# A four-layer image network: group norms' deviation moved to ScalarE, layer 1's front split and taken two images ahead

## The chip, the cores and the metric

The kernel runs on one core of a Trainium2 chip. The core has five engines that work from queues of their own: TensorE (PE, matrix products and transposes), VectorE (DVE), ScalarE (ACT), GpSimd (POOL) and SyncE (SP), which here issues all DMA transfers. An engine takes its instructions in order; an instruction waits on semaphores for the results of other engines, and everything behind it on its engine waits with it. The metric is device time in microseconds (us) of one execution.

## The reference

The input is 16 images of 192 channels by 32 x 32 points in float32. Four layers follow, each of the form `x = x + layer(group_norm(x))` with 32 groups of 6 channels. A group norm takes the mean and the variance over a group's channels and all points, and gives `(x - mean) / sqrt(var + 1e-5)`; "the deviation" below is the factor `(var + 1e-5) ** -0.5`.

- Layer 0 is an mLSTM block over the 1024 points as a sequence, then a 3 x 3 convolution, then a batch norm over all images and a leaky ReLU.
- Layer 1 is a Mamba block: layer norm, input projection to 384 channels and a gate, a causal convolution of width 4, SiLU, a selective scan with 16 states, gating, output projection, `skip_scale * xf` added, layer norm, projection.
- Layer 2 is a depthwise 3 x 3 convolution, batch norm over all images, clip to 0..6.
- Layer 3 is a vision Mamba with four scan directions per image beside a depthwise branch.

The recurrence that takes most of the time is, per state n and channel d, `h = exp(dt * A[d, n]) * h + dt * x * B[n]`, with `y += h * C[n]`.

The batch norm of layer 0 needs all images, so its leaky ReLU and the sum with x are done when layer 1 begins an image; the layer 1 group norm comes right after it. That beginning is called the front.

## The kernel before

Channels lie on partitions: 192 channels as two tiles of 96 (`m`), 384 as three of 128 (`t`). The 1024 points are two halves of 512. Layer 0 runs over all images first, then layers 1 and 2 together, then layer 3.

The scan of layers 1 and 3 (`scan_run`) goes over units, a unit being one half of one image (and direction), and over the 16 states of each: one pair is a step. Layer 1 has 32 steps an image, 512 in all; layer 3 has 2048. In a step ScalarE multiplies the transposed input by B (L966, tile `xbt`) and makes the decays (L986, `da`, five buffers), TensorE transposes the products into PSUM (L994, L997, `xb`, three buffers), VectorE runs three scan instructions (L1010, `h`), GpSimd multiplies by C (L1017), and TensorE adds up the result over states by transposes into PSUM (L1028, `y`). The row of C comes by DMA, broadcast to all partitions (`cb`, L968, four buffers).

All other work of layers 1 to 3 is written as generators and woven into the scan by `Side`. Each task has a kind, a start and an end, counted in steps; at every third of a step `tick` advances a task so far that its share of yields fits the time gone. A `Wait(n)` in a generator keeps it from going on for n steps. The tile framework then orders each engine's instructions and adds the semaphores.

In layer 1 image b begins at step `at = 32 * b`. Its neighbours' work is woven in: `prep` (projection to dt, B, C, and the transposes for the next unit), `gate` (gated output of the unit just done), `out` (output projection of image b-1), `silu` (the gate z of image b from its normalized input `xn`), `front` (for image b+1), `tail` (image b-1: layer norm, projection, sum with x1, group norm for layer 2), `conv` (causal convolution of image b+1, ending in a SiLU), and `layer 2` (image b-1). A SiLU on ScalarE needs another table of functions; `silu` (L1280s) loads it and then loads the table with logarithm and exponential again, so it is three instructions (L1283 twice, L1284).

The front of one image (`layer1_front`) has these parts: load x (`x1`, one buffer) and the layer 0 result (`xf`, one buffer) by DMA; batch norm's scale and shift on ScalarE (L1233), leaky ReLU (L1234) and sum (L1235) on VectorE; store of the sum to `self.x1`; group norm; the normalized image into `xf` (L1240) and its store to `self.xf1`; layer norm into `xn`, which takes x's buffer; projection and store of `xin` in DRAM, from which `conv` reads shifted copies (`rep`). `out` loads the stored `xf1` into the tile `xt` (one buffer), and `tail` works in that tile to the end of its group norm (`xpad`, L1351).

`group_norm` (L344 to L370) takes statistics per channel on VectorE (L351, L352), averages means over a group with a tiny matrix product (L355), takes deviations of means and a second moment (L357 to L362), averages again (L365), and makes the deviation: VectorE adds epsilon (L367), GpSimd raises to the power -0.5 (`pow_mhalf`, L309). It is used by layer 0's image (L541), layer 1's front and tail, and layer 3's front. `pow_mhalf` stays in use for batch norms.

Of the kernel before, what the change touches and what calls it, by code (L numbers as in the profile page):

```python
# [10 lines left out]
F32 = mybir.dt.float32  # L11
AF = mybir.ActivationFunctionType
# [4 lines left out]
ADD, SUB, MUL, MAX, MIN, POW = ALU.add, ALU.subtract, ALU.mult, ALU.max, ALU.min, ALU.pow  # L17

C = 192
HP = 96  # L20
DI = 384
S = 1024
# [6 lines left out]
EPS = 1e-5  # L29
# [160 lines left out]
def halves(n=S, step=512):  # L190
    return [slice(i, i + step) for i in range(0, n, step)]


def finish(steps):

    while True:
        try:
            next(steps)
        except StopIteration as end:
            return end.value  # L200
# [74 lines left out]
class Program:  # L275
# [68 lines left out]
    def group_norm(self, pool, psum, x):  # L344

        nc = self.nc
        st = pool.tile([HP, 2, 2, 6], F32, name="gnst")
        mv = pool.tile([HP, 2, 2], F32, name="gnmv")
        for m in range(2):
            for i, h in enumerate(halves()):  # L350
                nc.vector.bn_stats(st[:, m, i], x[:, m, h])  # L351
            nc.vector.bn_aggr(mv[:, m], st[:, m].rearrange("p a b -> p (a b)"))  # L352
            yield 1
        ps = psum.tile([128, 512], F32, name="mm")
        nc.tensor.matmul(ps[:HP, :2], self.k("group", HP), mv[:, :, 0], start=True, stop=True)  # L355
        mean = pool.tile([HP, 2], F32, name="gnmean")
        nc.vector.tensor_copy(mean, ps[:HP, :2])  # L357
        d = pool.tile([HP, 2], F32, name="gnd")
        nc.vector.tensor_tensor(d, mv[:, :, 0], mean, SUB)
        q = pool.tile([HP, 2], F32, name="gnq")  # L360
        nc.vector.tensor_tensor(q, d, d, MUL)
        nc.vector.tensor_tensor(q, q, mv[:, :, 1], ADD)  # L362
        yield 1
        ps = psum.tile([128, 512], F32, name="mm")
        nc.tensor.matmul(ps[:HP, :2], self.k("group", HP), q, start=True, stop=True)  # L365
        r = pool.tile([HP, 2], F32, name="gnr")
        nc.vector.tensor_scalar(r, ps[:HP, :2], EPS, None, ADD)  # L367
        self.pow_mhalf(r)
        yield 1
        return mean, r, d  # L370

# [698 lines left out]
    def layer12(self):  # L1070
        tc = self.tc
        with (
            tc.tile_pool(name="w1", bufs=1) as wp,
            tc.tile_pool(name="s1", bufs=2) as sp,
            tc.tile_pool(name="b1", bufs=2) as bp,
            tc.tile_pool(name="d1", bufs=3, space=DRAM) as dp,
            tc.tile_pool(name="ps1", bufs=2, space=PSUM) as psum,
        ):
            self.layer1_weights(wp, dp, psum)
            self.rep = 18 * (W + 2), 6  # L1080
            self.stats = wp.tile([HP, 2, 2 * self.nb, 6], F32, name="stats")
            self.image = {b: {} for b in range(self.nb)}
            side, units = Side(), []
            w_x = [self.w_x[:, t] for t in range(3)]

            def prep(u):
                xt = bp.tile([128, 4, DI], F32, name="xtok", bufs=1)
                xc = self.image[u.b]["xc"]
                rows = yield from self.scan_rows(xc[:, :, 512 * u.half : 512 * u.half + 512], w_x, 1, bp, dp, psum)
                yield from self.scan_prep(u, rows, 0, xc, xt, True, self.w_dt, bp, psum)  # L1090

            carry = [wp.tile([128, NS, 3], F32, name=f"carry{i}") for i in range(2)]
            for b in range(self.nb):
                for half in range(2):
                    c = carry[b % 2]
                    u = Unit(b, half, False, False, c if half else None, None if half else c)
                    u.neg_a = lambda t, n: self.neg_a[:, t * NS + n : t * NS + n + 1]
                    u.finish = lambda y, u=u: self.layer1_sum(u, y, bp)
                    units.append(u)
            for b in range(self.nb):  # L1100
                at = 2 * NS * b
                side.add("prep", prep(units[2 * b + 1]), at + 1, at + 13)
                if b:
                    side.add("gate", self.layer1_gated(units[2 * b - 1], bp, psum), at + 2, at + 3.5)
                    side.add("out", self.layer1_out(b - 1, bp, psum), at + 3.5, at + 8)
                side.add("silu", self.layer1_gate(b, bp, psum), at + 8, at + 12.5)
                if b + 1 < self.nb:
                    side.add("front", self.layer1_front(b + 1, sp, bp, psum), at + 12.5, at + 20)
                if b:
                    side.add("tail", self.layer1_tail(b - 1, sp, bp, dp, psum), at + 13.5, at + 25)  # L1110
                side.add("gate", self.layer1_gated(units[2 * b], bp, psum), at + 18, at + 21)
                if b + 1 < self.nb:
                    side.add("conv", self.layer1_conv(b + 1, bp, psum), at + 20, at + 26)
                if b:
                    side.add("layer 2", self.layer2(b - 1, bp, psum), at + 25.5, at + 34)
                if b + 1 < self.nb:
                    side.add("prep", prep(units[2 * b + 2]), at + 26, at + 30)
            finish(self.layer1_front(0, sp, bp, psum))
            finish(self.layer1_conv(0, bp, psum))
            finish(prep(units[0]))  # L1120
            self.scan_run(units, side, bp, psum)
            finish(self.layer1_gated(units[-1], bp, psum))
            finish(self.layer1_out(self.nb - 1, bp, psum))
            finish(self.layer1_tail(self.nb - 1, sp, bp, dp, psum))
            finish(self.layer2(self.nb - 1, bp, psum))
            self.batch_norm(sp, "2gamma", "2beta", self.bn2)
# [95 lines left out]
    def layer1_front(self, b, sp, bp, psum):  # L1222

        nc = self.nc
        x = bp.tile([HP, 2, S], F32, name="x1", bufs=1)
        nc.sync.dma_start(x, self.ins["x"][b].rearrange("(m p) t -> p m t", p=HP))
        xf = bp.tile([HP, 2, S], F32, name="xf", bufs=1)
        nc.sync.dma_start(xf, self.y0[b].rearrange("(m p) t -> p m t", p=HP))
        yield Wait(1)
        for m in range(2):  # L1230
            for h in halves():
                v = xf[:, m, h]
                nc.scalar.activation(v, v, AF.Identity, bias=self.bn0[:, m, 1:2], scale=self.bn0[:, m, 0:1])  # L1233
                nc.vector.scalar_tensor_tensor(v, v, 0.01, v, MUL, MAX)  # L1234
                nc.vector.tensor_tensor(x[:, m, h], x[:, m, h], v, ADD)  # L1235
                yield 0.5
        nc.sync.dma_start(self.x1[b], x)
        mean, r, _ = yield from self.group_norm(sp, psum, x)
        for m in range(2):
            nc.vector.tensor_scalar(xf[:, m], x[:, m], mean[:, m : m + 1], r[:, m : m + 1], SUB, MUL)  # L1240
        nc.sync.dma_start(self.xf1[b], xf)
        yield 1
        xn = x
        for h in halves():
            yield from self.layer_norm(
                bp, psum, [xf[:, m, h] for m in range(2)], [xn[:, m, h] for m in range(2)],
                self.k("ones192", HP), HP, 512,
            )
        for t in range(3):
            for h in halves():  # L1250
                ps = psum.tile([128, 512], F32, name="mm")
                for m in range(2):
                    nc.tensor.matmul(
                        ps, self.w_in[:, m, t * 128 : (t + 1) * 128], xn[:, m, h], start=m == 0, stop=m == 1
                    )
                o = bp.tile([128, 512], F32, name="o")
                nc.scalar.activation(o, ps, AF.Identity, bias=self.b_in[:, t : t + 1])
                nc.sync.dma_start(self.xin[b % 2][t][:, 3 + h.start : 3 + h.stop], o)
                yield 1.7
        self.image[b]["xn"] = xn  # L1260
# [450 lines left out]
```

## Time and profile before

| | us |
|---|---|
| median of three timed runs | 17368.59 |
| the three runs | 17350.56, 17368.59, 17390.61 |
| profiled execution's own time | 17403.5 |
| its span, first to last instruction | 17401.7 |
| first and last scan of layer 1 | 3943.8, 7529.7 |
| first and last scan of layer 3 | 7767.7, 17332.3 |

| engine | busy us | share of the span |
|---|---|---|
| PE | 15749.6 | 91% |
| DVE | 13122.0 | 75% |
| ACT | 11873.6 | 68% |
| POOL | 11450.8 | 66% |

How to read the lines shown below. A line of a view by tile or line gives the kernel's line, engine, operation, names as `out<-in`, how many there are, and minimum/median/maximum duration in ns; below it stand the engine's idle time ahead of these, by what ended it, and the time that others waited for them, with counts. A line of the timeline gives start and duration in us, then the same names, merged for neighbours alike, and in brackets the idle time of the engine before it and what ended that. A line of the windows gives each engine's busy time in a stretch. Matrix products overlap in the pipeline, so a busy PE is not one at its peak.

### The profile page before, as it was taken

Reading aid. Unit: us, or ns where it says so; the run is one execution under the profiler, and the core shown is the slowest. Engines: PE = TensorE matmul, PEld = TensorE weight load, DVE = VectorE, ACT = ScalarE, POOL = GpSimd, SP = SyncE. Lnnn points to the kernel's source line nnn. Section 1 sums busy time; section 2 is a strip of 40 time slices with the busy share of each in tenths; the row PEclk is TensorE's granted clock in tenths of the full one; section 3 lists DMA queues with packets and bytes.
Section 4 is the critical chain, followed back from the end, with each engine's and each line's share of the span. In section 5 each row is a group of like instructions: output and inputs, shape, how many; then the busy total and the mean of one; then the engine's idle time right before and its main releaser. Section 6 shows DMA issues by size and latency. Waiting matters only on the chain. (4 is left out here: it accounts for less than half of the span.)

```text
span 17401.7 us, 263068 instructions
## 1 busy us (share of the span) xinstructions
PE 15749.6 (91%) x99452; PEld 11013.2 (63%) x99452; DVE 13122.0 (75%) x14859; ACT 11873.6 (68%) x19637; POOL 11450.8 (66%) x5555
## 2 busy tenths in 40 slices
PE   8998988888988899979899999999999999999998
PEld 4444444435555555547777777777777777777777
DVE  4444444437777777749889888888888888888888
ACT  3222322327666666648888888888888888888888
POOL 3333333425555555538788788888878888888888
PEclk8889998989999999989999999999999999999999
DMA  1111111123333343433333333323333333333332
GB/s 51 42 40 44 44 43 44 47 63 107 114 110 110 113 118 116 118 99 103 90 99 107 93 96 101 107 83 99 107 98 92 99 108 88 96 105 102 88 98 67
DMA packets 890141, 1544.65 MB, mean 89 GB/s; under 512 B 83472, under 2 KB 314653, under 8 KB 879530
## 3 DMA queue, kind: packets, MB, share of 16 engines
q1 hardware_dynamic: 888874, 1527.81, 30.3%
q8 instruction: 788, 12.91, 0.3%
q14 instruction: 479, 3.92, 0.1%
HBM read 1284.22 MB, written 243.27 MB: 88 GB/s over the span
## 5 line engine op out<-in xcount | busy, mean ns | idle before, releaser
L1017 POOL TENSOR_TENSOR h<-h,cb 128x1536 f32<-128x1536 f32 x2560 | 8872.8, 3469 | 1432.0 <-DVE h L1010 902.9
L986 ACT ACTIVATE da<-dt,neg_a 128x512 f32<-128x512 f32 x7680 | 5267.0, 714 | 1752.0 <-DVE h L1010 1687.3
L1010 DVE TENSOR_TENSOR_SCAN h<-da,carry,xb 128x512 f32<-128x512 f32 x3840 | 4652.4, 1262 | 657.1 <-PE xb L997 596.2
L1028 PE MATMUL y<-const,h 128*128 128x128 f32 x30720 | 4717.9, 276 | 128.3 <-DVE ysum L1468 54.0
L1010 DVE TENSOR_TENSOR_SCAN h<-da,xb 128x512 f32<-128x512 f32 x3840 | 4440.6, 1202 | 388.7 <-PE xb L997 270.7
L994 PE MATMUL xb<-const,xbt 128*128 128x128 f32 x23040 | 4074.6, 282 | 422.5 <-DVE h L1010 269.3
L966 ACT ACTIVATE xbt<-ut,bt 128x384 f32<-128x384 f32 x7680 | 4174.4, 603 | 246.4 <-PE xb L994 244.3
L994 PEld LDWEIGHTS xb<-const,xbt 128*128 128x128 f32 x23040 | 2757.2, 143 | 1815.5 <-issue 643.8
L1028 PEld LDWEIGHTS y<-const,h 128*128 128x128 f32 x30720 | 3684.9, 143 | 322.8 <-issue 265.4
L997 PE MATMUL xb<-diag,ut 128*128 128x128 f32 x15360 | 3016.4, 279 | 0.0
L997 PEld LDWEIGHTS xb<-diag,ut 128*128 128x128 f32 x15360 | 2383.5, 195 | 63.1 <-issue 63.1
L830 POOL TENSOR_TENSOR hs<-h,mhm 128x384 f32<-128x384 f32 x128 | 108.5, 848 | 1685.1 <-DVE den L835 1290.5
L1016 POOL COPY carry<-h 128x3 f32<-128x3 f32 x1280 | 250.5, 196 | 1220.1 <-DVE h L1010 964.7
L976 POOL TENSOR_TENSOR diag<-const,bt 128x512 f32<-128x512 f32 x640 | 680.8, 1064 | 550.5 <-PE xb L997 362.1
L705 POOL TENSOR_TENSOR e<-e,const 128x1536 f32<-128x1536 f32 x128 | 439.9, 3437 | 288.9 <-DMA e<-row 273.0
L520 PE MATMUL conv<-ya,w_conv 128*64 128x512 f32 (+1 forms) x1152 | 543.9, 656 | 66.1 <-DMA ya<-yrows 62.2
L916 PE MATMUL mm<-dbl,w_dt 45*128 45x512 f32 x960 | 532.8, 639 | 33.6 <-DVE v L1490 16.2
L711 ACT ACTIVATE e<-e 128x1536 f32<-128x1536 f32 x128 | 189.7, 1482 | 417.7 <-POOL e L706 417.4
L854 DVE TENSOR_TENSOR ht<-sz,mm 128x384 f32<-128x384 f32 x128 | 70.7, 552 | 519.5 <-PE mm L851 519.5
L1171 PE MATMUL mm<-rep,t_dw 96*32 96x512 f32 x2304 | 433.5, 614 | 23.5 <-DMA rep<-xr 17.3
L779 PEld LDWEIGHTS num<-v,p 128*128 128x128 f32 x3072 | 389.3, 201 | 102.2 <-issue 77.9
L920 DVE SCALAR_TENSOR_TENSOR dt<-lnsq,mm 128x512 f32<-128x512 f32 x480 | 322.0, 671 | 171.9 <-ACT lnsq L919 171.9
(272 smaller groups left out, 17910.1 us busy)
## 6 DMA issues: line engine op xcount, KB each, us to landing
cb<-row SPq DMA_DIRECT2D x2560, 256.0 KB
rep<-xr SPq DMA_DIRECT2D x384, 331.0 KB
e<-row SPq DMA_DIRECT2D x128, 768.0 KB
rep<-xin SPq DMA_DIRECT2D x384, 256.0 KB
rep<-xr SPq DMA_DIRECT2D x384, 228.8 KB
x<-x SPq DMA_DIRECT2D x48, 768.0 KB
xr<-xin SPq DMA_DIRECT2D x48, 612.5 KB
xr<-xpad SPq DMA_DIRECT2D x32, 867.0 KB
```

The source lines that it names most:

```text
L520: nc.tensor.matmul(o, self.w_c2[:k, t, c0 : c0 + o.shape[0]], src[:k, r0 : r0 + 16, dx : dx + W], start=t == 0, stop=t == 14, skip_group_c ...
L705: nc.gpsimd.tensor_tensor(k.e, k.e, self.k0("mask")[:, None, :].to_broadcast([128, NH, 128]), ADD)
L916: nc.tensor.matmul(ps, w_dt[:, t * 128 : (t + 1) * 128], dbl, start=True, stop=True)
L966: nc.scalar.activation(t[:, c], u.ut[:, c], AF.Copy, scale=u.bt[:, c, n : n + 1])
L976: nc.gpsimd.tensor_tensor(d, ident[:, None, :].to_broadcast([128, 4, 128]), u.bt[:, 3, n : n + 4][:, :, None].to_broadcast([128, 4, 128]), ...
L986: nc.scalar.activation(da[i, t], u.dt[:, t], AF.Exp, scale=u.neg_a(t, n))
L994: in_order(nc.tensor.transpose(xb[i, t][:, c * 128 : (c + 1) * 128], xbt[i][:, c, t * 128 : (t + 1) * 128], ident))
L997: in_order(nc.tensor.matmul(xb[i, t][:, 384:], u.ut[:, 3, t * 128 : (t + 1) * 128], u.diag[n // 4][:, n % 4], start=True, stop=True, skip_ ...
L1010: nc.vector.tensor_tensor_scan(hv, dv, xv, 0.0 if first else u.carry_in[:, n, t : t + 1], MUL, ADD)
L1017: nc.gpsimd.tensor_tensor(h[i], h[i], u.c.pop(n)[:, None, :].to_broadcast([128, 3, 512]), MUL)
L1028: in_order(nc.tensor.matmul(u.y[:, j], h[i][:, t, c * 128 : (c + 1) * 128], ident, is_transpose=True, start=n == 0 and j % 4 == 0, stop=n ...
L1171: self.nc.tensor.matmul(ps[32 * g : 32 * g + 32], blocks[:, g * side + r], seen, start=r == 0, stop=r == side - 1, skip_group_check=True,)
```

## The change

1. `group_norm` makes the deviation on ScalarE: `Ln(v + eps)`, then `Exp(-0.5 * that)`. The averaged variance is read from PSUM by the first of them.
2. `layer1_front` now ends with the store of the normalized image, and leaves `xf` for later. What followed it becomes a task of its own, `layer1_xin`. The layer norm's output gets the tile `x1`; the sum x is loaded into the tile `xt`, which `out` and `tail` use as well. The front yields 1 instead of 0.5 for each of its four pieces.
3. In `layer12` the front runs for image b+2 in steps 26.5 to 35 of image b (image 1's in steps 2 to 10 of image 0), and `xin` for image b+1 in steps 13 to 20. Several other tasks have their starts and ends moved: `prep`, `silu`, `tail`, `gate`, `conv`, `layer 2`.

```diff
@@ group_norm
         r = pool.tile([HP, 2], F32, name="gnr")
-        nc.vector.tensor_scalar(r, ps[:HP, :2], EPS, None, ADD)
-        self.pow_mhalf(r)
+        nc.scalar.activation(r, ps[:HP, :2], AF.Ln, bias=self.k("eps", HP))
+        nc.scalar.activation(r, r, AF.Exp, scale=-0.5)
         yield 1
@@ layer12
                 at = 2 * NS * b
-                side.add("prep", prep(units[2 * b + 1]), at + 1, at + 13)
+                side.add("prep", prep(units[2 * b + 1]), at + 0.5, at + 12)
                 if b:
                     side.add("gate", self.layer1_gated(units[2 * b - 1], bp, psum), at + 2, at + 3.5)
                     side.add("out", self.layer1_out(b - 1, bp, psum), at + 3.5, at + 8)
-                side.add("silu", self.layer1_gate(b, bp, psum), at + 8, at + 12.5)
+                elif self.nb > 1:
+                    side.add("front", self.layer1_front(1, sp, bp, psum), 2, 10)
+                side.add("silu", self.layer1_gate(b, bp, psum), at + 8, at + 13)
                 if b + 1 < self.nb:
-                    side.add("front", self.layer1_front(b + 1, sp, bp, psum), at + 12.5, at + 20)
+                    side.add("xin", self.layer1_xin(b + 1, bp, psum), at + 13, at + 20)
                 if b:
-                    side.add("tail", self.layer1_tail(b - 1, sp, bp, dp, psum), at + 13.5, at + 25)
-                side.add("gate", self.layer1_gated(units[2 * b], bp, psum), at + 18, at + 21)
+                    side.add("tail", self.layer1_tail(b - 1, sp, bp, dp, psum), at + 14, at + 26)
+                side.add("gate", self.layer1_gated(units[2 * b], bp, psum), at + 18.5, at + 22)
                 if b + 1 < self.nb:
-                    side.add("conv", self.layer1_conv(b + 1, bp, psum), at + 20, at + 26)
+                    side.add("conv", self.layer1_conv(b + 1, bp, psum), at + 18, at + 24.5)
+                    side.add("prep", prep(units[2 * b + 2]), at + 24.5, at + 29.5)
                 if b:
-                    side.add("layer 2", self.layer2(b - 1, bp, psum), at + 25.5, at + 34)
-                if b + 1 < self.nb:
-                    side.add("prep", prep(units[2 * b + 2]), at + 26, at + 30)
+                    side.add("layer 2", self.layer2(b - 1, bp, psum), at + 26, at + 35)
+                if b + 2 < self.nb:
+                    side.add("front", self.layer1_front(b + 2, sp, bp, psum), at + 26.5, at + 35)
             finish(self.layer1_front(0, sp, bp, psum))
+            finish(self.layer1_xin(0, bp, psum))
@@ layer1_front
-        x = bp.tile([HP, 2, S], F32, name="x1", bufs=1)
+        x = bp.tile([HP, 2, S], F32, name="xt", bufs=1)
...
-                yield 0.5
+                yield 1
...
         nc.sync.dma_start(self.xf1[b], xf)
+        self.image[b]["xf"] = xf
         yield 1
-        xn = x
+
+    def layer1_xin(self, b, bp, psum):
+
+        nc = self.nc
+        xf = self.image[b].pop("xf")
+        xn = bp.tile([HP, 2, S], F32, name="x1", bufs=1)
         for h in halves():
             yield from self.layer_norm(
```

## The prediction

> **What bounds the kernel now.** I read the page first: TensorE is busy 91% of 17401.7 us, VectorE 75%, ScalarE 68%, GpSimd 66%, so no engine is full and order matters. Group norms carry little work; what counts is who waits at them. The view of the group norm's deviation, limited to layer 0 (200 to 3700 us), answers that:
>
> ```profile
> L309 POOL TENSOR_TENSOR gnr<-gnr,const x15: 685/694/700, 200.3 to 3455.0; 96x2 f32<-96x2 f32 x15
>   POOL gnr L309: 55.5, 15
>   PE mm L377: 94.9, 14
> ```
>
> The power takes 0.69 us, but VectorE sits idle 55.5 us in 15 images for it (3.7 each) and TensorE 94.9 us for the normalized image behind it. The same view of layer 3's loop (7700 us on) has VectorE idle 23.7 us in 15 images (1.58 each). One layer 0 image, VectorE and GpSimd by time, shows why:
>
> ```profile
> 1372.98 0.14 DVE L367 TENSOR_SCALAR gnr<-mm 96x2 f32<-96x2 f32 x1
> 1373.05 0.54 DVE L854 TENSOR_TENSOR ht<-sz,mm 128x384 f32<-128x384 f32 x1
> 1376.55 3.80 DVE L543 TENSOR_SCALAR x<-x,gnmean,gnr 96x1024 f32<-96x1024 f32 x2 [2.96 <-POOL gnr L309]
> ...
> 1373.11 2.75 POOL L706 TENSOR_TENSOR e<-e,uw 128x1536 f32<-128x1536 f32 x1
> 1375.82 0.69 POOL L309 TENSOR_TENSOR gnr<-gnr,const 96x2 f32<-96x2 f32 x1
> ```
>
> The power stands behind a 2.75 us product in GpSimd's queue.
>
> Layer 1 is the larger part. Each of its images repeats nearly alike, 226 to 232 us from scan to scan in the timeline. I cut image 7 at its scan steps 0, 5, 12, 18, 27 and 32 (32 steps an image) and took the windows:
>
> ```profile
> core 0: us, PE busy (x) PEld busy (x) DVE busy (x) ACT busy (x) POOL busy (x), PEclk, DMA share, GB/s
> 5510.40:5536.60 26.20, 24.13 (x173) 18.86 (x172) 19.98 (x21) 19.40 (x32) 20.51 (x12) 0.93 0.22 65
> 5536.60:5585.00 48.40, 46.30 (x261) 31.33 (x260) 34.45 (x37) 32.49 (x55) 30.20 (x20) 1.00 0.16 48
> 5585.00:5628.90 43.90, 33.95 (x198) 24.89 (x197) 37.71 (x46) 30.77 (x47) 23.25 (x12) 0.92 0.31 91
> 5628.90:5703.00 74.10, 65.61 (x365) 38.92 (x363) 57.72 (x65) 44.79 (x68) 37.92 (x15) 1.00 0.59 176
> 5703.00:5741.60 38.60, 37.11 (x228) 20.59 (x227) 24.32 (x27) 29.51 (x51) 19.70 (x8) 1.00 0.50 141
> ```
>
> TensorE's idle time is the wall less its busy time: 2.1, 2.1, 9.9, 8.5 and 1.5 us. The hole is in the third row, steps 12 to 17, where VectorE is at 86%. It is the present front of the next image:
>
> ```profile
> 5595.28 4.67 DVE L1235 TENSOR_TENSOR x<-x,xf 96x512 f32<-96x512 f32 x4 [1.81 <-DMA x<-x]
> 5599.87 1.87 DVE L351 BATCH_NORM_STATS2 gnst<-x 96x6 f32<-96x512 f32 x3
> 5611.81 2.24 DVE L1240 TENSOR_SCALAR xf<-x,gnmean,gnr 96x1024 f32<-96x1024 f32 x2 [0.70 <-POOL gnr L309]
> ```
>
> Step 13 takes 13.7 us against 3.3 to 7 in quiet ones: after its three scans VectorE waits 1.81 us for x, then does sums and statistics while the next scan, and TensorE behind it, stand. ScalarE is meanwhile in silu with its two table loads (1.28 + 2.77 + 1.28 = 5.3 us), so the two holes partly cover each other.
>
> **What the Trainium skill says.** "SBUF — State Buffer", Who interferes with whom: a VectorE instruction with two SBUF inputs, or in a 2-port mode, and a GpSimd one that reads SBUF exclude each other for a whole instruction. The trace agrees: the first of the four sums at L1235 took 2.86 us, the others 0.68; gnq at L361 took 2.42 us once in image 7 instead of 0.13; xpad at L1351 3.94 instead of 0.79. "ScalarE: Activation LUTs", What ACT_TABLE_LOAD costs: about 1283 ns a load; the trace has 1283. Same page, Table sets: logarithm and exponential share one set, so the new pair should switch nothing. The built program agrees: inside the loops no load is added; only ahead of layer 0 there is one more.
>
> **The change part by part**, against the profiled execution's 17403.5 us (span 17401.7). The three timed runs' median is 17368.6, 35 below, and the sum is carried over as a difference.
>
> *Deviation on ScalarE.* Per group norm one 0.145 us VectorE instruction (L367) and a 0.69 us GpSimd power go, and two tiny ScalarE instructions come; the nearest row, the 128x12 pair at L839 and L840, takes 0.21 us each. 64 times 0.42 us is 27 us of ScalarE, which is idle 32% of the time.
>
> Layer 0: in the program's order the pair stands after L840 and ahead of the exponential at L711, where ScalarE waited 2.34 us in the image shown, so it is covered; bare it costs 0.4 an image. TensorE's order is otherwise the one of before. The deviation is there some 0.5 us after L840 begins, not behind L706. The most to win is the whole idle 3.7 us an image. The least is nothing: L543 can wait for GpSimd's 2.75 us product at the shared port instead. I take 2.0, as the power's own 0.69 certainly leaves the chain: 15 x 2.0 = -30 (0 to -55).
>
> Layer 3: orders are the same but for the group norm; the pair sits between copies of step-ahead input (L966) and xpad moves behind the third scan. VectorE's 1.58 us a front is at stake; ScalarE's place costs at most one 0.6 us instruction ahead of it. I take -1.3 x 15 = -20 (-24 to +10).
>
> Start: one table load more, +1.3.
>
> *Front split and moved.* From steps 13 to 15 go, on VectorE, four sums and their wait (6.5), four statistics (2.5), small pieces (about 1), L1240 and its wait (2.9): 13 us. In exchange xin's layer norm (L379, L389), formerly in steps 16 to 18, starts at 13, and silu is now bare: VectorE has about 3.5 us of scans in step 14 beside 5.3 of ScalarE. Decays (L986) are made ahead in five buffers, over a step, which hides most of it. Of the 9.9 us hole I let silu keep 2 and win 8 (4.6 if silu is wholly bare; 9.9 if not at all).
>
> The new place is steps 27 to 33, beside layer 2's matmuls, with TensorE idle 1.5 us in 38.6 but VectorE idle 14.3. Into it come four sums (2.7), four statistics (2.5), aggregates and 96x2 pieces (1), two normalizations (1.6): 7.8 us. The leaky ReLU (L1234, four of 0.67) and its ScalarE half stay near steps 18 and 19. VectorE's queue has scans behind each piece and TensorE waits for scans, so what VectorE's spare time doesn't cover is paid. The sums stand at four places now, each open to a port wait; before, one of 2.2 us was paid. I take +3 (0 if all is covered, +14.7 if 7.8 is bare with two port waits of 3.45).
>
> DMAs: x now loads into xt on SP after xpad's store to xr and prep's row store, ahead of layer 2's replicas; x1d and xf1d stores and the next y0 load keep their sizes. SP holds the C rows (cb) too, four buffers deep, and those queue behind any wait. The load took 7.1 us from issue (5588.2) to the release of L1235 (5595.3). From xpad in step 25 to the first sum, late in step 27, there are some 9 us, so I price lateness at 0 (up to +3, like the 1.8 paid now; layer 2's replicas would be late next). xf1d's store, the row store and xt's load at steps 1 to 2 have until step 5.
>
> The tail's group norm (step 24, 12 us) loses GpSimd's power between scans: -1 (0 to -2). Conv, prep and silu of xc move earlier by about two steps; steps 18 to 26 keep their TensorE work, so 0 (-4 to +4).
>
> Image: -8 + 3 - 1 = -6. The loop has 15 images' fronts in both kernels (image 0 gains a second, image 14 loses its own): 15 x -6 = -90.
>
> Sum: -30 - 20 - 90 + 1 = -139: 17403.5 becomes 17264, the median **17230 us** (ratio 0.992).
>
> **Rivals.**
>
> *Whole hole won*: front covered at its new place and silu by the lead of the decays: -9.9 - 1 and one or two of rebalancing, -12 an image, -180; with -65 of group norms 17124. For it: VectorE's idle 14.3. Against: port waits.
>
> *Only the norms*: layer 1 trades one hole for another, -50: 17319.
>
> *Slower: the front is bare where it lands.* Steps 27 to 33 have no idle TensorE; each VectorE microsecond ahead of a scan is paid (+14.7) and of the old hole only 4.6 comes back, as silu loses its cover: +10 an image, +150 - 50 = +100: 17469. It decides once layer 1 loses over (35 + 50)/15 = 5.7 us an image. For it: today's front shows just such a bunching. Against: the program's order spreads the pieces between scans there, where today eight stand in one gap.
>
> *Nothing*: port waits take the place of the power and layer 1 trades evenly: 17369. The change does do what it says: in the built program no power is left in a group norm's chain.
>
> **How the numbers follow.** My case (17170 to 17300) 0.44; whole hole 0.14; only norms 0.10; nothing 0.10; slower 0.22. 0.2% (35 us) is about what measuring this kernel can tell from no change. Faster: 0.44 + 0.14 + most of the norms' case = 0.66; same 0.12; slower 0.22. Range: from 17080, past the whole-hole case (its bounds reach 17070), to 17450, short of the slower case's centre.
>
> **What would show it.** Right: image to image about 224 us in layer 1; the window of steps 12 to 17 some 8 us shorter; no 13 us step there; L543's wait in layer 0 under 2 us and named for ScalarE; layer 3 shorter by about 1 us an image. Wrong: steps 27 to 33 longer by over 8 us with VectorE full, sums at 3 us (port) or waiting for x, scans waiting for decays behind silu, or cb late behind SP's stores.

## The result, and the profile after

The changed kernel takes **17205.5 us**, the median of four runs (17199.5 to 17211.1), against 17367.3 for the kernel before on the same chip: ratio 0.9906, 95% interval 0.9889 to 0.9923. It is faster by 162 us, or 0.94%.

Where the time went, from the first and last scan of each layer in the two profiles:

| us | before | after | difference |
|---|---|---|---|
| layer 0, to the first scan of layer 1 | 3943.8 | 3876.0 | -67.8 |
| layer 1, first to last scan | 3585.9 | 3480.9 | -105.0 |
| between | 238.0 | 232.8 | -5.2 |
| layer 3, first to last scan | 9564.6 | 9547.6 | -17.0 |
| end | 69.4 | 71.7 | +2.3 |
| span | 17401.7 | 17209.0 | -192.7 |

The two profiles differ by 31 us more than the medians: the profiled execution of before was 36 us above its median, that of after (17210.8) 5 us. Layer 0 varies from profile to profile: of the changed kernel and those told of below, the nine that have the new deviation and leave its small operands as they are took 3846 to 3901 us, mean 3870; the two with the old deviation (before and `e2`) took 3944 and 3926.

The view by tile of the group norm's deviation, in layer 0 (200 to 3700 us), after:

```profile
L543 DVE TENSOR_SCALAR x<-x,gnmean,gnr x30: 799/1927/3236, 209.0 to 3396.7; 96x1024 f32<-96x1024 f32 x30
L367 ACT ACTIVATE gnr<-mm,const x15: 240/241/258, 202.5 to 3393.8; 96x2 f32<-96x2 f32 x15
L368 ACT ACTIVATE gnr<-gnr x15: 187/203/204, 203.2 to 3394.1; 96x2 f32<-96x2 f32 x15
...
  ACT gnr L368: 5.3, 12
...
  PE mm L377: 54.2, 16
```

The logarithm and the exponential take 0.24 and 0.20 us. VectorE's wait falls from 55.5 to 5.3 us, and TensorE's from 94.9 to 54.2. In layer 3 VectorE's wait of 23.7 us is gone altogether.

Layer 1's image 7, cut at the same scan steps 0, 5, 12, 18, 27 and 32, in the view of windows:

```profile
core 0: us, PE busy (x) PEld busy (x) DVE busy (x) ACT busy (x) POOL busy (x), PEclk, DMA share, GB/s
5398.30:5431.70 33.40, 27.26 (x189) 18.68 (x188) 28.47 (x27) 20.49 (x36) 21.63 (x13) 0.95 0.34 101
5431.70:5478.70 47.00, 45.25 (x264) 31.40 (x263) 34.35 (x36) 31.66 (x54) 30.31 (x20) 1.00 0.13 45
5478.70:5515.20 36.50, 32.90 (x196) 23.02 (x195) 27.85 (x31) 32.33 (x51) 23.86 (x12) 1.00 0.23 66
5515.20:5590.60 75.40, 67.32 (x370) 40.25 (x369) 55.31 (x63) 46.37 (x72) 34.46 (x14) 0.95 0.59 180
5590.60:5625.00 34.40, 30.83 (x209) 19.66 (x208) 30.87 (x35) 25.43 (x46) 19.18 (x7) 0.95 0.52 147
```

TensorE's idle time, wall less busy, is now 6.1, 1.8, 3.6, 8.1 and 3.6 us, where it was 2.1, 2.1, 9.9, 8.5 and 1.5. The hole in the third row gave back 6.3. The first and the last row, where the front lands now, took 6.1 of idle time. What remains of the gain in this image is shorter TensorE busy time: 207.1 us before, 203.6 after. Layer 1 as a whole, in the view of windows, shows the same: TensorE's idle time falls from 365.6 to 321.4 us, by 44, and its busy time from 3220.3 to 3159.5, by 61, for 19090 and 19088 matrix products. The granted clock is no cause for that, as it is 0.97 in both (in image 7 it rises in rows 1 and 3 of the windows and falls in rows 4 and 5); what shortens the busy time is not followed here.

Over images 2 to 13 the stretches went from 25.3, 48.3, 44.1, 73.0 and 38.6 us to 30.5, 47.0, 36.5, 74.2 and 34.6, and images 1 to 14 from 229.3 to 222.4 each. The last stretch is shorter although the front is in it, as it has fewer matrix products (in image 7 209 for 228): work of the retimed neighbours left it.

The front at its new place, VectorE by time, image 7, steps 27 to 33:

```profile
5594.73 1.11 DVE L1239 TENSOR_TENSOR xt<-xt,xf 96x512 f32<-96x512 f32 x1
...
5596.37 3.35 DVE L1239 TENSOR_TENSOR xt<-xt,xf 96x512 f32<-96x512 f32 x1
...
5629.82 3.21 DVE L359 TENSOR_TENSOR gnd<-gnmv,gnmean 96x2 f32<-96x2 f32 x1
...
5636.95 4.61 DVE L1244 TENSOR_SCALAR xf<-xt,gnmean,gnr 96x1024 f32<-96x1024 f32 x2 [0.42 <-ACT gnr L368]
```

And GpSimd by time, the products beside them:

```profile
5595.25 3.92 POOL L1017 TENSOR_TENSOR h<-h,cb 128x1536 f32<-128x1536 f32 x1
...
5629.59 3.43 POOL L1017 TENSOR_TENSOR h<-h,cb 128x1536 f32<-128x1536 f32 x1
...
5636.86 3.42 POOL L1017 TENSOR_TENSOR h<-h,cb 128x1536 f32<-128x1536 f32 x1
```

The sum of 5596.37 ends at 5599.72, just after the product of 5595.25 (5599.17). The 96x2 difference at 5629.82, otherwise 0.15 us, ends at 5633.03, with the product of 5629.59 (5633.02). The normalization of 5636.95 starts 0.09 after a product and takes 3.89 + 0.8. All three look like waits at the port that VectorE shares with GpSimd, and the next scans stand behind each. `e4` below tests this for the 96x2 pieces; for the sums and the normalization no run does.

### The profile page after: what moved, and what is told of

Read it like the earlier page. It is cut to its first block, busy times and chain, and to the rows that moved or that the text cites. A ratio compares the mean times of both kernels' runs of the same rounds, so it can differ in the third digit from the quotient of the medians.

```text
span 17209.0 us, 263098 instructions
## 1 busy us (share of the span) xinstructions
PE 15665.1 (91%) x99452; PEld 10971.6 (64%) x99452; DVE 13151.7 (76%) x14795; ACT 11873.1 (69%) x19766; POOL 11417.3 (66%) x5491
## 3 DMA queue, kind: packets, MB, share of 16 engines
q1 hardware_dynamic: 888874, 1527.81, 29.6%
## 4 chain that ended last, share of the span: by engine, by line
PE 32%; DVE 10%; ACT 9%; issue 4%; POOL 2%; DMA 1%; SPq 0%; DVEq 0%; POOLq 0%; ACTq 0%
PE y L1028 9%; PE xb L994 8%; DVE h L1010 7%; PE xb L997 5%; PE mm L1175 3%; ACT da L986 3%; ACT xbt L966 3%; POOL h L1017 2%; PE mm L887 1%; PE mm L916 1%; PE mm L1604 1%; PE mm L1624 1%; PE mm L936 1%; PE mm L1589 1%; PE mm L1678 1%
## 5 line engine op out<-in xcount | busy, mean ns | idle before, releaser
L1010 DVE TENSOR_TENSOR_SCAN h<-da,carry,xb 128x512 f32<-128x512 f32 x3840 | 4653.1, 1263 | 752.9 <-PE xb L997 661.9
L1028 PE MATMUL y<-const,h 128*128 128x128 f32 x30720 | 4698.6, 275 | 124.4 <-DVE ysum L1478 54.2
L1010 DVE TENSOR_TENSOR_SCAN h<-da,xb 128x512 f32<-128x512 f32 x3840 | 4445.5, 1203 | 424.5 <-PE xb L997 267.4
L916 PE MATMUL mm<-dbl,w_dt 45*128 45x512 f32 x960 | 536.9, 643 | 34.6 <-DVE v L1500 15.7
L1175 PE MATMUL mm<-rep,taps 128*32 128x512 f32 x3072 | 424.2, 607 | 24.5 <-DMA rep<-xr 15.2
```

Source lines behind the costliest of these rows:

```text
L916: nc.tensor.matmul(ps, w_dt[:, t * 128 : (t + 1) * 128], dbl, start=True, stop=True)
L1010: nc.vector.tensor_tensor_scan(hv, dv, xv, 0.0 if first else u.carry_in[:, n, t : t + 1], MUL, ADD)
L1028: in_order(nc.tensor.matmul(u.y[:, j], h[i][:, t, c * 128 : (c + 1) * 128], ident, is_transpose=True, start=n == 0 and j % 4 == 0, stop=n ...
L1175: self.nc.tensor.matmul(ps[32 * g : 32 * g + 32], blocks[:, g * side + r], seen, start=r == 0, stop=r == side - 1, skip_group_check=True,)
```

## The experiments

Ratios are to the kernel before on the same chip, with 95% intervals. The runs lie on three chips, on which the kernel before took 17339.6 to 17346.5 us, 21 to 28 less than beside the changed kernel. So where a run is compared with the changed kernel, two figures are given: the difference of the two times as they stand, and, called "net", the difference of their gains over the kernel before. Layer 1 is first to last scan in each kernel's profile.

### The two parts alone

`e1` has only the first hunk of the diff, `e2` all but that hunk.

> The kernel before with the deviation on ScalarE alone, front and times as they were. My theory (gains of the two parts add; layer 0 was worth 30 us, layer 3 20, layer 1's group norms little): about 55 us under before. The profile after shows layer 0 shorter by 68 and layer 3 by 17, so if those are the change's own and not the clock's, 85 to 100 us under before. Rival (the norms give all and the moved front nothing): about 160 us under before. L543's idle time in layer 0 must fall from 55.5 to about 5 us as in the changed kernel.

> The changed kernel with the deviation made by VectorE and GpSimd again. My theory: 70 to 100 us under before, all of it in layer 1, image to image about 223 us, layer 0 and layer 3 as before. Rival (the gain in layer 1 is the norms' own): within 35 us of before. A third case: the front's deviation, at its new place behind GpSimd's product, costs layer 1 more than it did at the old place, and less than 50 us are left.

Measured: e1 17245.4, ratio 0.9944 (0.9932 to 0.9957); e2 17245.7, ratio 0.9941 (0.9928 to 0.9953). Each brings 99 us, and the two together 162, not 198. In e1 layer 1 takes 3531.2 (-55), in e2 3462.3 (-124), in the changed kernel 3480.9: with the front moved, the deviation on ScalarE brings layer 1 nothing. In e1 the gain shows in steps 18 to 26, 73.0 to 67.0 us an image, where the tail's group norm lies; in e2 and in the changed kernel these steps take 74.1 and 74.2.

The two normalizations of an image, each behind its own deviation, show in part why the gains do not add. Busy time and idle time ahead of them in the view by line, whole program (32 instructions each), us:

| | before | e1 | e2 | changed |
|---|---|---|---|---|
| tail (`xpad`) | 58.7 + 3.2 | 27.5 + 1.1 | 24.5 + 11.2 | 29.1 + 3.6 |
| front (`xf`) | 35.1 + 10.9 | 52.6 + 1.5 | 24.7 + 44.0 | 44.4 + 10.2 |

In the tail the new deviation saves 33 us in e1, but the move and the new times alone (e2) save 26 of them. At the front's new place the new deviation takes 34 us of waiting away and puts 20 us of longer normalizations in its place.

### Is the front bare at its new place?

`e8` leaves out the four sums of the front, so that layer 0's result is not added to x.

```diff
-                nc.vector.tensor_tensor(x[:, m, h], x[:, m, h], v, ADD)
+                pass
```

> The changed kernel with the four sums of the front (L1239) left out, so that layer 0's result is not added; statistics and normalization stay. It prices VectorE's time at the front's new place: the sums and their port waits take 5.8 us an image. If what lands in steps 27 to 33 is covered, an image gets shorter by under 2 us; if it is bare, by 4 to 6 us. My forecast took 3 of up to 14.7 us as paid, a fifth, so I expect 1 to 3 us, 15 to 45 us in all.

Measured: 17111.4 (two runs), ratio 0.9866 (0.9848 to 0.9884), 94 us under the changed kernel, net 73. Layer 1 takes 3410.1, 71 us less, where I expected 15 to 45. Layer 0 is 30 us shorter in this profile though nothing was edited there. The last rows of the view of windows for e8's image 7, same cuts:

```profile
5452.23:5527.73 75.50, 67.34 (x372) 40.54 (x370) 55.38 (x64) 46.67 (x72) 34.37 (x14) 0.95 0.59 180
5527.73:5556.76 29.03, 28.90 (x208) 18.93 (x207) 25.37 (x31) 25.33 (x45) 18.65 (x7) 1.00 0.61 173
```

All other stretches stay; steps 27 to 31 fall by 5.0 us an image (34.6 to 29.6) and TensorE's idle time in them to 0.1. The sums take 1.11 + 3.35 + 0.66 + 0.68 = 5.8 us. So these are paid nearly in full, in spite of VectorE's idle time elsewhere in the stretch: VectorE by time shows no gap from 5589.45 to 5605.0, where they stand, and its next scan after that waits 2.16 us for TensorE's products.

`e4` takes away the port waits of the small pieces alone: the small pieces are made with at most one operand in SBUF, the other in PSUM, which takes one instruction more.

```diff
-        d = pool.tile([HP, 2], F32, name="gnd")
-        nc.vector.tensor_tensor(d, mv[:, :, 0], mean, SUB)
+        d, dp, dd = pool.tile([HP, 2], F32, name="gnd"), ps[:HP, 2:4], ps[:HP, 4:6]
+        nc.vector.tensor_tensor(d, mv[:, :, 0], ps[:HP, :2], SUB); nc.vector.tensor_tensor(dp, mv[:, :, 0], ps[:HP, :2], SUB)
...
-        nc.vector.tensor_tensor(q, d, d, MUL)
-        nc.vector.tensor_tensor(q, q, mv[:, :, 1], ADD)
+        nc.vector.tensor_tensor(dd, d, dp, MUL)
+        nc.vector.tensor_tensor(q, mv[:, :, 1], dd, ADD)
```

> The changed kernel, with the group norm's small pieces (L359 to L362) reading at most one operand from SBUF and the other from PSUM, one small instruction more; the program's order is almost the one of the changed kernel. In the changed kernel gnd at L359 took 3.2 us in step 0 of images 3 to 8 and gnq at L361 2.2 us in step 25 of each, instead of 0.13. If that is the wait at the port shared with GpSimd, both fall to under 0.3 us; layer 1 is then shorter by up to 2 us in step 25 of 15 images and by 3 in step 0 of 8, some 30 to 55 us in all. Rival (the long ones wait for something else, such as a semaphore counted as busy): durations stay and time is within 20 us of the changed kernel.

Measured: 17080.9, ratio 0.9848 (0.9835 to 0.9862), 125 us under the changed kernel, net 102, where I had expected 30 to 55. Two of the lines, whole program; first the changed kernel, then e4:

```profile
L361 DVE TENSOR_TENSOR gnq<-gnd x64: 126/157/3346, 35.0 to 16218.5; 96x2 f32<-96x2 f32 x64
...
L359 DVE TENSOR_TENSOR gnd<-gnmv,gnmean x64: 145/158/3215, 34.8 to 16218.3; 96x2 f32<-96x2 f32 x64
```

```profile
L361 DVE TENSOR_TENSOR mm<-gnd,mm x64: 144/152/161, 35.0 to 16086.0; 96x2 f32<-96x2 f32 x64
...
L359 DVE TENSOR_TENSOR gnd<-gnmv,mm x64: 136/142/147, 34.7 to 16085.8; 96x2 f32<-96x2 f32 x64
```

No one of these 256 instructions takes over 0.17 us now. In the changed kernel the three at L359, L361 and L362 together waited 110 us (what they took over 0.15 us each, where above 0.5): 4 in layer 0, 62 in layer 1, 44 in layer 3, which my expectation left out. Before it was 4, 37 and 44, and e1 and e2 have 37 and 62 in layer 1, so the 25 us more come with the front's move and the new times. Layer 1 fell by 80 us in e4, layer 3 by 32, layer 0 by 19, of which the last is within what layer 0 varies. "SBUF — State Buffer", Who interferes with whom, in the Trainium skill says that a VectorE instruction with at most one SBUF input, outside the modes with two ports, does not contend with GpSimd; this pair of traces agrees.

The changed kernel holds an experiment of its own. In images 3 to 8 the difference (L359) starts just behind a product and takes 3.21 us, and the first normalization 3.9; steps 0 and 1 take 18.5 to 19.6 us. In images 9 to 14 the program's order on VectorE puts the small pieces together two scans after step 0; L359 takes 1.29, the normalization 0.81, and the two steps take 12.1 us. Images 3 to 8 take 225 to 228 us, 9 to 14 between 218 and 222. The order of other pieces differs too, so this is not the price of the waits alone.

### What do the neighbours' new times bring?

`e3` keeps front and `xin` at their new places and gives all other tasks their old starts and ends.

> The changed kernel with the starts and ends of prep, silu, tail, gate, conv and layer 2 as before; norms on ScalarE, front two images ahead and xin at 13 to 20 stay. My theory (the split and the move bring the gain, the neighbours' times little, 0 plus or minus 4 us an image): within 60 us of the changed kernel, and steps 12 to 17 still about 37 us. Rival (the retimed neighbours bring layer 1's gain): about 100 us over the changed kernel.

Measured: 17109.8, ratio 0.9865 (0.985 to 0.988), 96 us *under* the changed kernel, net 73; layer 1 takes 3391.4, 90 less. Steps 18 to 26 fall from 74.2 to 59.8 us; 12 to 17 and 27 to 31 give back 3.5 and 4.4. The last three rows of the windows, image 7 of e3:

```profile
5440.33:5480.32 39.99, 39.03 (x212) 25.46 (x210) 34.95 (x39) 36.36 (x57) 25.08 (x12) 1.00 0.23 66
5480.32:5540.18 59.86, 57.18 (x340) 35.26 (x339) 47.85 (x53) 37.65 (x64) 33.60 (x14) 1.00 0.63 202
5540.18:5577.66 37.48, 34.78 (x237) 21.42 (x236) 28.61 (x36) 30.19 (x48) 19.51 (x8) 1.00 0.60 167
```

So some 10 us of what steps 18 to 26 lose is TensorE work that now lies in the two rows beside them (57.2 us busy, 67.3 in the changed kernel). Over the whole image TensorE is busy as long as in the changed kernel (203.1 and 203.5 us); what is won is idle time, 13.4 us for 23.1, and in steps 12 to 17, where the old hole was, 1.0 us of it is left.

Which times? `e6` has conv and the prep behind it at the old times, `e7` tail and the second gate, `e10` all four.

```diff
-                    side.add("tail", self.layer1_tail(b - 1, sp, bp, dp, psum), at + 14, at + 26)
-                side.add("gate", self.layer1_gated(units[2 * b], bp, psum), at + 18.5, at + 22)
+                    side.add("tail", self.layer1_tail(b - 1, sp, bp, dp, psum), at + 13.5, at + 25)
+                side.add("gate", self.layer1_gated(units[2 * b], bp, psum), at + 18, at + 21)
...
-                    side.add("conv", self.layer1_conv(b + 1, bp, psum), at + 18, at + 24.5)
-                    side.add("prep", prep(units[2 * b + 2]), at + 24.5, at + 29.5)
+                    side.add("conv", self.layer1_conv(b + 1, bp, psum), at + 20, at + 26)
+                    side.add("prep", prep(units[2 * b + 2]), at + 26, at + 30)
```

> The changed kernel with conv at 20 to 26 and the next unit's prep at 26 to 30 as before; the other new times stay. In the changed kernel step 18 takes 15.4 us, with VectorE 2.9 us waiting for the tail's x1 loads, which stand in SP's queue behind xin's stores and conv's shifted copies. If conv's early start is what crowds steps 18 to 26: those fall from 74 to about 62 us an image and the kernel comes to within 40 us of the one with all old times, 17110 to 17150. If tail or gate do it: it stays within 40 us of the changed kernel, 17170 to 17240.

> The changed kernel with tail at 13.5 to 25 and the second gate at 18 to 21 as before; conv and prep keep the new times. The other half of the same question: if conv crowds the steps, it stays within 40 us of the changed kernel; if the tail's later start does it (its residual sum and the leaky ReLU meeting in step 18), steps 18 to 26 fall from 74 to about 62 us.

> The changed kernel with conv, the second prep, tail and the second gate at their old times together, the first prep, silu and layer 2 at the new ones. Each pair alone brought nothing. Theory A (the tail's first half must be ahead of xin's stores and the convolution behind the tail; both are needed): the gain of all old times together, 17110 (17090 to 17150), steps 18 to 26 at about 60 us. Theory B (the first prep, silu or layer 2 carry it): 17200 to 17270.

Measured: e6 17266.0, ratio 0.9955 (0.994 to 0.997), slower than the changed kernel and outside both of my cases; e7 17211.9, ratio 0.9925 (0.9911 to 0.9938), not told apart from it; e10 17105.7, ratio 0.9859 (0.9845 to 0.9874), the whole gain of e3. So the two pairs have to go back together: the first prep, silu and layer 2 add nothing that can be measured. The time lies elsewhere than I expected, though: steps 18 to 26 take 66.0 us in e10, not 60, and the steps after them 37.0 (e3: 59.8 and 39.0).

What the scans of images 2 to 13 (1152 of them) waited for: VectorE's idle time ahead of L1010, us and times, before:

```profile
  PE xb L997: 157.5, 198
  ACT da L986: 8.5, 10
  ACT xbt L966: 4.2, 9
```

the changed kernel:

```profile
  PE xb L997: 199.9, 170
  ACT da L986: 46.4, 66
  ACT xbt L966: 19.6, 13
  POOL carry L1016: 11.1, 12
```

and e10:

```profile
  PE xb L997: 157.6, 155
  POOL carry L1016: 11.1, 12
  ACT xbt L966: 8.4, 12
  ACT da L986: 0.9, 2
```

With the new times scans wait 38 us more for decays and 42 us more for TensorE's products than before. In e10 the decays are in time again. In e6 the decays stay late (45.8 us), in e7 the products get later (245.5): each half mends one of the two and leaves or worsens the other. The scans' waits are not the whole account: in e6 they add up to 240 us for 278 in the changed kernel, and an image is still 5 us longer. VectorE waits more at other pieces there, 86.0 us from 4200 to 7200 us for the tail's loads of x1 (L1354), for 59.9.

One candidate for what makes them late was the tail's residual. In step 18 of the changed kernel VectorE stands at the sum with x1, and the queue of SP waits to load it, since the `o` buffers are still held by stores of `xin`. SP's waits, 5478 to 5590 us:

```profile
SPq L1346 <- DMA xin<-o: 4.6, 2, 3.2
```

`e9` gives these loads a tile of their own, and pays for it with one replica buffer.

```diff
-            self.rep = 18 * (W + 2), 6
+            self.rep = 18 * (W + 2), 5
...
-                o.append(bp.tile([128, 512], F32, name="o"))
+                o.append(bp.tile([128, 512], F32, name="res"))
```

> The changed kernel, with a tile of their own (two buffers) for the two residual loads that the tail adds after its projection, where it shares the two o buffers with the stores of xin; the replicas of the convolutions get five buffers for six to make room. Theory A (in step 18 the residual loads are late because they wait for the o buffers, which the stores of xin hold: issued at 5.1 and 9.3 us into the step, the second sum at 15): steps 18 to 26 fall from 74.2 to about 67 us an image, the wait for the residual at the sums from 60 us to under 20 in the loop, time 17205 - 100 = 17105 (17070 to 17150). Theory B (the loads are late because SP stands at other transfers, or the neighbours' new times cost by something else): 17190 to 17220, the steps unchanged.

Measured: 17196.7, ratio 0.9914 (0.9897 to 0.993), not told apart from the changed kernel. In the changed kernel VectorE's idle time ahead of the tail's sums (L1354), images 2 to 13, was 50.2 us:

```profile
  DMA o<-x1d: 50.2, 27
```

In e9 it is none at all, and steps 18 to 26 shorten by 3.0 us an image, not 7. Scans still wait 33.5 us for decays and 180.5 for products. Theory A falls as it was put: the wait was there and was removed, and the time did not follow. The missing sixth replica buffer hides part of the answer, as TensorE now waits 22 us (21 times) for the replicas of layer 2, 2.4 in the changed kernel; but the late decays, which the edit doesn't touch, remain. That the two pairs have to go back together is shown; the chain that makes the decays late in between is not followed to its start.

### What does the bare silu cost?

`e12` leaves out the SiLU of the gate in layer 1 with its two table loads; the gate enters unactivated.

> The changed kernel without the SiLU of the gate in layer 1 and its two table loads (the gate is then not SiLU'd), which takes 5.3 us of ScalarE an image near step 14. The prediction let this SiLU keep 2 us an image of the old hole: then time falls by 2 x 16 = 32, to 17175, and steps 12 to 17 by 2 us. If it is hidden behind the decays made ahead: 17200. If it is wholly bare: -5.3 x 16 = -85, 17120.

Measured: 17138.5 (two runs), ratio 0.9879 (0.9857 to 0.9902): 67 us less, net 39 (its interval still touches that of the changed kernel, 0.9889 to 0.9923). Layer 1 falls by 67, or 4.2 an image, of 5.3 that ScalarE spends. The third and fourth rows of the windows, image 7 of e12:

```profile
5481.69:5522.50 40.81, 38.72 (x210) 25.45 (x209) 34.95 (x37) 32.08 (x54) 24.85 (x12) 1.00 0.31 95
5522.50:5587.83 65.33, 59.53 (x355) 37.04 (x354) 50.63 (x57) 41.62 (x65) 33.42 (x13) 0.97 0.58 185
```

The gain isn't where silu stands. Steps 12 to 17 get *longer* (36.5 to 40.8) and take more work (TensorE busy 38.7 us for 32.9); steps 18 to 26 fall from 74.2 to 65.1. The program's order moves with the edit, so this is not silu's price in its place alone.

### Is there a better version?

`e5` joins e3 and e4; `e11` adds e9's edit to e5.

> The kernel with the neighbours' old times (17110) and the group norm's small pieces with PSUM operands (which took 125 us off the changed kernel). My theory (port waits and the crowding of steps 18 to 26 are separate holes): the two gains add to within a third, 16990 to 17040, about 320 us under before. Rival (both remove the same waiting of layer 1): no lower than 17080 in layers 0 and 3's share only, that is 50 us under the kernel with old times.

> All old times for the neighbours, the group norm's small operands in PSUM, and the residual's own tile. The residual's wait at the sums is only 18.6 us in the loop with the old times. If that wait is paid: 17059 - 15 = 17044. If it is not, or if five replica buffers cost what it brings: 17050 to 17075.

Measured: e5 **17059.2**, ratio 0.9837 (0.9823 to 0.985): the best kernel here, 287 us under the kernel before and 146 under the changed one, net 126. Its two gains, net 73 and 102, overlap: it falls between my two cases, and the operands in PSUM bring 51 us beside the old times. e11 took 17163.1, ratio 0.9894 (0.9879 to 0.9909), 104 worse than e5, outside both expectations: steps 27 to 31 go from 38.2 to 44.2 us. What the missing sixth buffer does there is not a wait of layer 2's products for replicas, which is at most 3.5 us from 4200 to 7200 us, nearly all of layer 1. In the same time VectorE waits 36.8 us for TensorE's products in the next unit's preparation (L937), for 8.1 in e5, and over images 2 to 13 the four sums of the front take 6.0 us an image for 3.6. How one buffer leads to that is not followed, and no run has five buffers alone.

## Why the prediction was right, and where its steps were not

The forecast was 17230 and -139 us; measured, 17205.5 and -162. Sign, size and range hold, in part by luck, as errors of the steps cancel. Step by step:

- **Layer 0, -30 (0 to -55): too small,** and outside its range. Mean of nine profiles 3870 against 3935 for the old deviation, -65. VectorE's wait falls by 50 and L543's own time by 4 (62.7 to 58.7 us in all); TensorE's idle time falls by 54 and its busy time by 14 (3460.7 to 3446.5). Part of this is the spread of layer 0: in e2, with the old deviation, VectorE's wait is 43.3, not 55.5. I took half of the wait since L543 might instead stand at the port behind the same product. The timeline that I showed had a hint: L543's two took 3.80 us there for 2 x 0.8, so a port wait was paid *beside* the wait for the power already. With the power gone it did not grow.
- **Layer 3, -20: within its range, but not told apart from less.** -17 in the changed kernel, -18 in e1; but e2, whose layer 3 is that of before, took 9553.8, 11 us less than before too. ScalarE waits 39.5 us in 15 fronts for the averaged variance ahead of its logarithm; what that costs is in these figures.
- **Steps 12 to 17, -8: right,** -7.6; no step there is over 9 us. The scans behind silu wait 1.12 and 0.45 us for decays, close to the 2 that I let it keep, as VectorE by time shows for the changed kernel:

```profile
5489.94 3.44 DVE L1010 TENSOR_TENSOR_SCAN h<-da,xb 128x512 f32<-128x512 f32 x3 [1.12 <-ACT da L986]
...
5493.83 1.22 DVE L1010 TENSOR_TENSOR_SCAN h<-da,xb 128x512 f32<-128x512 f32 x1 [0.45 <-ACT da L986]
```

Silu's whole price is more than that, up to 4.2 an image by e12: with it gone, steps 18 to 26 get shorter, which is not followed here.

- **The new place, +3 (0 to +14.7): mis-sized, by up to two.** Idle TensorE in steps 27 to 31 and 0 to 4 grew by 6.1 us in image 7 (4.4 over images 2 to 13), and e8 puts 5.0 on the sums alone. I set VectorE's 14.3 us of idle time against 7.8 us of new work; but none of it lay where the sums stand. I had priced no port wait in the middle value; one of 3.35 and one of 3.21 are there in this image.
- **The tail's group norm, -1 (0 to -2): mis-sized.** Alone, the new deviation takes 6.0 us from steps 18 to 26, adds 2.0 to steps 12 to 17, and takes 3.6 from the image (55 us in 15). The table of e1 and e2 puts 33 us of this beside the tail's normalization, 31 of them in its own duration: I priced the wait for the power and not the normalization's own duration. In the changed kernel none of it is left.
- **Retimed neighbours, 0 (-4 to +4): this is the step that failed.** The stretch itself did as I said (73.0 to 74.2; idle 8.5 to 8.1), for I compared it only with before. But I did not ask what the moved front and the new deviation would do at the old times: there the stretch takes 59.8 us, some 10 of the difference being TensorE work that lies beside it, and the image has 13.4 us of TensorE idle time for 23.1. The new times bring late decays and products and cost 73 (net) to 96 us in all.
- **Lateness of x, 0: right.** No sum at L1239 waits for its load in the changed kernel; with the old times they would (26.9 us in e3).

The image's sum, -6, came out at -6.9, but not by its terms, and this is luck: I added up idle time of TensorE, which fell by only 2.3 us an image (23.1 to 20.8 over images 2 to 13); its busy time, for which the sum had no term, fell by 4.2. Of the rivals, "nothing" and "only the norms" are out. "The front is bare where it lands" was right that the sums are paid, but not on 14.7 us in all, and wrong on the old hole, which came back at 7.6 and not 4.6. "The whole hole won", -245 us, is close to what the front's move and the norms are worth without the retimed neighbours: -235 in e3, -234 in e10, and in e3 the hole's idle time did fall from 9.9 to 1.0.

## What to carry to other kernels

An engine's idle time in a stretch is no cover by itself: what stands in its queue ahead of an instruction that the bound engine waits for was paid here almost in full (5.0 of 5.8 us), though the stretch had held 14 us of idle time before. When a piece leaves a stretch, measure first with its neighbours where they were: here the retiming that came with the move cost 73 to 96 us, and as undoing either half of it alone gained nothing, one half at a time would not have found it. Compare whole images too, not one stretch, since moved work changes a stretch's time without changing the sum. And look for tiny instructions with a maximum twenty times their median: taking 96x2 operations from a port by an operand in PSUM was worth 102 to 125 us in the changed kernel, and 51 with the old times.

## What was not expected of the hardware

- A 96x2 VectorE operation of 0.15 us took 3.21 us when it met a GpSimd product of 3.43, and ended within 0.02 us of it; the longest took 3.45 (L362). Of the 192 such operations at L359, L361 and L362 in the changed kernel 48 took over 0.5 us, 110 us in all beyond their usual 0.15; with an operand in PSUM, none did.
- A group norm's deviation on ScalarE took 0.24 + 0.20 us from PSUM, against 0.12 to 0.15 + 0.69 on VectorE and GpSimd, where the second part stood behind a 2.75 us product in the image shown.
- One replica buffer less, five for six, with a tile of their own for the residual loads, cost 104 us (e11 against e5), and TensorE's waits for replicas at layer 2 do not show it (at most 3.5 us from 4200 to 7200 us).
